# Layer 0 self attention of a four-layer decoder by half sequences, with 32-row and 32-column TensorE tiles

## The chip, the cores and the metric

The kernel runs on one core of a Trainium2 chip, in one launch. The metric is the device time of one execution in microseconds (us); lower is better. The profiled execution is one execution with the hardware profiler on, and its own time is given beside its span.

## The reference

A decoder of four layers works on `x` of shape (16, 128, 128): 16 sequences of 128 tokens with 128 channels, float32. Each layer has a self attention, a cross attention and a feed-forward stage, all of different kinds, with a layer norm before each stage and a residual after it. The change touches the first of the twelve stages alone. Cut to that stage (16 heads of width 8, causal softmax, and a decay that depends on the distance of two tokens and is multiplied in after the softmax):

```python
x = x + attn(layernorm(x))

def attn(x):
    q, k, v = split(x @ W_attn, 3)             # (16, 128, 128) each, 16 heads of 8
    S = q @ k.T / sqrt(8)                      # per sequence and head, 128 x 128
    P = softmax(where(causal, S, -inf))
    y = (P * decay) @ v                        # decay is lower triangular, a constant
    return concat_heads(y) @ W_proj
```

## The kernel before

All 16 sequences lie in SBUF from start to end, tokens on the partitions, in G = 4 groups of GB = 4 sequences: `X[g]` is 128 x (4 x 128). The twelve stages run one after another. Each opens its own PSUM banks (eight in all, split into rings by name: `x`, `S`, `P`, `O`) and its own SBUF pools. Tiles come from rotating pools, and a framework puts in the semaphores. A scheduler of that framework fixes each engine's order of instructions when the kernel is built, so that every engine then works its own list strictly in order; the source order is not the order of the lists.

The stage is `l0_attn` (L470). `pre_norm` (L308) normalises all of `X`: statistics on VectorE (L286, L287), the scaling (L299), four transposes a group on TensorE (L276) and a copy out of PSUM on ScalarE (L317). Then, group by group:

- q and k for the whole group, channels on the partitions (L478), copied out by VectorE (L483, L485), and v, tokens on the partitions (L489, L497).
- For each sequence `expand_heads` (L462) makes `kexp` on GpSimd: the keys of the sequence, 16 times over, each copy with all channels but one head's set to zero (128 x 2048). With it one matmul over all 128 channels gives the scores of several heads at once.
- `small_head_attention` (L424) works a sequence in four units of 4 heads. In a unit TensorE puts the causal mask into a bank by a bfloat16 matmul (L433) and adds the scores (L440, 512 columns; a float32 matmul is two passes, each with a weight load). `softmax_unit` (L324) takes the row maximum on VectorE (`nmax`, L329) and four exponentials on ScalarE (L332), each with a running sum that is read out by an instruction of its own (ACTIVATION_READ_ACCUMULATOR). Four transposes on TensorE follow (L345), then the product with the decay on VectorE on the way out of PSUM (L348), then four matmuls with the transposed weights as the stationary operand and 8 columns of v as the moving one (L452).
- After the four units the division by the sums (L456, L503) and one transpose into `yT` (L509). After the four sequences the copy of `yT` (L511), the output projection (L514) and the residual (L322).

At the start of the program the bfloat16 constants, among them the causal mask, come through a wide float32 tile and a cast on GpSimd (L268); the scores wait for them.

Of the kernel before, what the change touches and what calls it, by code (L numbers as in the profile page):

```python
# [36 lines left out]
def _columns(sizes):  # L37
    at, out = 0, {}
    for name, n in sizes:
# [9 lines left out]
        ("decayT", 128),  # L49
        ("cumsum", 128),  # L50
        ("head8", 16),
        ("head16", 8),
        ("mod8", 8),
        ("head64", 2),
# [107 lines left out]
class Decoder:  # L162
# [145 lines left out]
    def pre_norm(self, transpose=True):  # L308
# [9 lines left out]
            xnT.append(dst)  # L318
        return xn, xnT

    def add_to_x(self, g, what):
        self.nc.vector.tensor_tensor(self.X[g], self.X[g], what, ALU.add)  # L322

# [143 lines left out]
        )  # L467
        return kexp

    def l0_attn(self, pool, _):  # L470
        nc = self.nc
        _, xnT = self.pre_norm()
        Wa, Wp = self.w["W_attn"], self.w["W_proj"]
        for g in range(G):
            qk = []
            for i in range(2):
                bank = self.ps()
                nc.tensor.matmul(  # L478
                    bank, lhsT=Wa[:, i * 128 : (i + 1) * 128], rhs=xnT[g], start=True, stop=True
                )  # L480
                sb = self.t(pool, (128, N), f"qk{i}")
                if i == 0:
                    nc.vector.tensor_scalar_mul(sb, bank, 1.0 / math.sqrt(8))  # L483
                else:
                    nc.vector.tensor_copy(sb, bank)  # L485
                qk.append(sb)
            v_ps = self.ps((T, GB, D))
            for b in range(GB):
                nc.tensor.matmul(  # L489
                    v_ps[:, b, :],  # L490
                    lhsT=xnT[g][:, b * T : (b + 1) * T],
                    rhs=Wa[:, 256:384],
                    start=True,
                    stop=True,
                )
            v = self.t(pool, (T, GB, D), "v")
            nc.vector.tensor_copy(v, v_ps)  # L497
            yT = self.ps()
            for b in range(GB):
                kexp = self.expand_heads(pool, qk[1], self.cst("head8"), b, 16)  # L500
                O, r = self.small_head_attention(pool, qk[0], kexp, v[:, b, :], b, True)
                y = self.t(pool, (T, D), "y")
                nc.vector.tensor_tensor(  # L503
                    y.rearrange("p (h d) -> p h d", h=16),
                    O,
                    r.unsqueeze(2).to_broadcast([T, 16, 8]),
                    ALU.mult,
                )
                nc.tensor.transpose(yT[:, b * T : (b + 1) * T], y, self.ident)  # L509
            yTs = self.t(pool, (D, N), "yT")  # L510
            nc.vector.tensor_copy(yTs, yT)  # L511
            o = self.ps((T, GB, D))
            for b in range(GB):
                nc.tensor.matmul(  # L514
                    o[:, b, :], lhsT=yTs[:, b * T : (b + 1) * T], rhs=Wp, start=True, stop=True
                )
            self.add_to_x(g, o)

    def context_T(self):
        for g in range(G):  # L520
# [882 lines left out]
    def run(self, stack):  # L1403
        self.setup(stack)
        with ExitStack() as inner:
            self.banks(inner, "c", x=8)
            self.context_T()
        heads = dict(x=2, S=2, P=2, O=2)
        moe = dict(x=2, S=2, P=2, O=2)
        todo = [  # L1410
            (self.l0_attn, 2, heads), (self.l0_xattn, 2, heads), (self.l0_ffn, 2, moe),
            (self.l1_attn, 2, heads), (self.l1_xattn, 2, heads), (self.l1_ffn, 2, dict(x=2, S=5, O=1)),
            (self.l2_attn, 2, dict(x=2, S=2, P=2, O=2)), (self.l2_xattn, 2, heads), (self.l2_ffn, 2, dict(x=3, S=3, O=2)),
            (self.l3_attn, 2, dict(x=2, S=4, O=2)), (self.l3_xattn, 2, dict(x=8)), (self.l3_ffn, 3, moe),
        ]
# [22 lines left out]
def constants():  # L1438
    import numpy as np

    p = np.arange(128)
    c = np.zeros((128, CONST_N), np.float32)
    half = np.zeros((128, HALF_N), np.float32)

    def put(name, a, columns=CONST, into=c):
        at, n = columns[name]
        a = np.asarray(a, np.float32).reshape(-1, n)
        into[: len(a), at : at + n] = a

# [8 lines left out]
    put("head8", p[:, None] // 8 == np.arange(16))  # L1458
    put("head16", p[:, None] // 16 == np.arange(8))
# [145 lines left out]
```

## Time and profile before

| | |
|---|---|
| runs, no profiler | 2403.79, 2404.2, 2407.95 us; median 2404.2 us |
| profiled execution, own time | 2406.38 us |
| its span in the trace | 2404.6 us |
| mean granted TensorE clock | 0.853 of full speed |
| busy share of the span | TensorE 81%, VectorE 58%, ScalarE 39%, GpSimd 24% |
| the stage in the trace | `kexp` of the first group starts at 31.51 us, the last residual of the stage (L322) at 246.42 us |
| instructions in the stage | 256 exponentials with 256 read-outs, 64 row maxima, 64 decay products, 16 `kexp` |

A busy time is the sum of the durations of the instructions of one engine, where overlaps count once. Matmuls are pipelined: the start of one to the start of the next says what it costs, and its duration is longer than that. PEclk is the TensorE clock that the throttle granted, as a share of full speed. What stands in brackets at the end of a row of the timeline is the engine's idle time before the row and what ended it.

### The profile page before, as it was taken

How to read it: one execution, taken by the hardware profiler on the slowest of the kernel's cores; microseconds unless marked ns; L12 is line 12 of the kernel's file. 1: busy time of each engine (PE TensorE's matmuls, PEld its weight loads, DVE VectorE, ACT ScalarE, POOL GpSimd, SP SyncE). 2: the span in 40 equal slices, each digit the busy share in tenths (PEclk: the TensorE clock that was granted, in tenths of full speed). 3: DMA queues.
4: the chain of work that ended last, by engine and by line, in shares of the span. 5: the costliest groups of instructions: out<-in, count | busy, mean ns of one | idle time of the engine just before them, and what ended most of it. 6: DMA issues, size and time to landing. Idle time of an engine off the chain costs nothing.

```text
span 2404.6 us, 25103 instructions
## 1 busy us (share of the span) xinstructions
PE 1941.3 (81%) x8660; PEld 1213.5 (50%) x8660; DVE 1387.8 (58%) x2650; ACT 936.6 (39%) x3012; POOL 569.6 (24%) x544
## 2 busy tenths in 40 slices
PE   6998787889889999977667668999964498328998
PEld 4666555357558887632212226777743355213443
DVE  4555365457656666456777764545455546884333
ACT  3444243246525555136343334445431143222333
POOL 2222131033200001415777752000001105610000
PEclk8888597869899999976887879999976677558999
DMA  4000000000000000000000000000000000000000
GB/s 147 1 1 1 1 1 1 33 3 1 1 1 1 1 1 29 2 0 0 1 0 1 0 33 1 1 1 1 1 31 0 0 1 0 0 0 0 5 5 9
DMA packets 11890, 19.08 MB, mean 8 GB/s; under 512 B 1499, under 2 KB 8795, under 8 KB 11379
## 3 DMA queue, kind: packets, MB, share of 16 engines
q1 hardware_dynamic: 11763, 17.49, 2.1%
q8 instruction: 68, 1.11, 0.2%
q14 instruction: 59, 0.48, 0.1%
HBM read 16.30 MB, written 1.05 MB: 7 GB/s over the span
## 4 chain that ended last, share of the span: by engine, by line
PE 67%; DVE 14%; POOL 9%; issue 6%; ACT 2%; DMA 0%; POOLq 0%; DVEq 0%; ACTq 0%; SPq 0%
PE ps_P L345 6%; POOL hC L1030 6%; PE ps_O L414 5%; PE ps_S L440 5%; PE ps_O L452 5%; PE ps_O L756 5%; PE ps_S L745 5%; PE ps_S L406 4%; DVE hs L1028 2%; PE ps_O L1031 2%; DVE xn L299 2%; PE ps_S L743 2%; PE ps_O L763 1%; PE ps_x L1109 1%; PE ps_x L854 1%
## 5 line engine op out<-in xcount | busy, mean ns | idle before, releaser
L332 ACT ACTIVATE P<-ps_S,nmax 128x128 f32<-128x128 f32 x1024 | 362.0, 367 | 295.9 <-DVE nmax L329 294.3
L329 DVE TENSOR_REDUCE nmax<-ps_S 128x4 f32<-128x512 f32 x256 | 176.5, 691 | 138.9 <-PE ps_S L745 77.9
L1031 PE MATMUL ps_O<-hC,consts 128*128 128x512 f32 x256 | 177.5, 794 | 93.6 <-POOL hC L1030 83.3
L1030 POOL TENSOR_TENSOR hC<-hs,Cw 128x512 f32<-128x512 f32 x128 | 205.3, 1622 | 91.8 <-DVE hs L1028 50.2
L332 ACT ACTIVATION_READ_ACCUMULATOR P<-ps_S,nmax 128x1 f32 x1024 | 209.1, 204 | 0.0
L1028 DVE TENSOR_TENSOR_SCAN hs<-dA,dBx 128x512 f32<-128x512 f32 x128 | 162.8, 1309 | 71.4 <-POOL dA L1024 71.4
L350 DVE COPY PT<-ps_P 128x512 f32<-128x512 f32 x224 | 154.1, 688 | 85.8 <-PE ps_P L345 84.3
L345 PE MATMUL ps_P<-consts,P 128*128 128x128 f32 x1024 | 200.8, 288 | 1.3 <-ACT P L332 0.7
L413 DVE TENSOR_TENSOR ehg<-eh,ps_P 128x512 f32<-128x512 f32 x128 | 86.6, 687 | 143.9 <-PE ps_P L411 99.4
L345 PEld LDWEIGHTS ps_P<-consts,P 128*128 128x128 f32 x1024 | 137.3, 158 | 53.7 <-ACT P L332 44.9
L408 ACT ACTIVATE eh<-ps_S,params 128x512 f32<-128x512 f32 x128 | 87.5, 687 | 184.7 <-PE ps_S L406 142.3
L1031 PEld LDWEIGHTS ps_O<-hC,consts 128*128 128x128 f32 x256 | 47.2, 224 | 192.4 <-POOL hC L1030 124.3
L745 PE MATMUL ps_S<-kexp,q 128*128 128x256 f32 x512 | 141.0, 381 | 0.0
L414 PE MATMUL ps_O<-ehg,w 128*128 128x512 f32 x256 | 136.4, 630 | 4.0 <-DVE ehg L413 4.0
L756 PEld LDWEIGHTS ps_O<-v,PT 128*128 128x128 f32 x1024 | 127.1, 191 | 19.8 <-DVE PT L350 13.5
L406 PE MATMUL ps_S<-xnT,w 128*128 128x512 f32 x256 | 133.3, 610 | 0.0
L756 PE MATMUL ps_O<-v,PT 128*128 128x64 f32 x1024 | 131.6, 271 | 0.2 <-DVE PT L350 0.2
L1022 ACT ACTIVATE dA<-dt,A 128x512 f32<-128x512 f32 x128 | 92.4, 722 | 83.5 <-DVE hs L1028 83.4
L1138 POOL TENSOR_TENSOR q_v<-q_v,q_e 128x512 f32<-128x512 f32 (+3 forms) x10 | 21.1, 2120 | 436.4 <-DVE q_e L1137 436.4
L322 DVE TENSOR_TENSOR x<-x,ps_x 128x512 f32<-128x512 f32 x32 | 21.9, 684 | 145.6 <-PE ps_x L1191 46.5
L745 PEld LDWEIGHTS ps_S<-kexp,q 128*128 128x128 f32 x512 | 87.0, 192 | 16.0 <-issue 3.2
L276 PE MATMUL ps_x<-consts,xn 128*128 128x128 f32 x176 | 42.0, 397 | 61.0 <-DVE xn L299 57.8
(395 smaller groups left out, 3831.7 us busy)
## 6 DMA issues: line engine op xcount, KB each, us to landing
w<-in_w_dram SPq DMA_DIRECT2D x2, 1792.0 KB
wide_consts<-in_half_dram SPq DMA_DIRECT2D x1, 1554.0 KB
x<-in_x_dram SPq DMA_DIRECT2D x4, 256.0 KB
c<-in_ctx_dram SPq DMA_DIRECT2D x4, 256.0 KB
w<-in_Wq_dram SPq DMA_DIRECT2D x2, 512.0 KB
w<-in_Wo_dram SPq DMA_DIRECT2D x2, 512.0 KB
out_dram<-x SPq DMA_DIRECT2D x4, 256.0 KB
consts<-in_consts_dram SPq DMA_DIRECT2D x1, 748.0 KB
```

The lines of the kernel that those rows point to most:

```text
L329: nc.vector.tensor_reduce(nmax, S, AX.X, ALU.max, negate=True)
L332: nc.scalar.activation(P[:, j, :], S[:, j, :], AF.Exp, bias=nmax[:, j : j + 1], accum_out=sums[:, j : j + 1],)
L345: nc.tensor.transpose(PT[:, j, :], P[:, j, :], self.ident)
L350: nc.vector.tensor_copy(out, PT)
L406: nc.tensor.matmul(h_ps, lhsT=W1(c), rhs=xnT[g], start=True, stop=True)
L414: nc.tensor.matmul(acc, lhsT=W2(c), rhs=hg, start=False, stop=c == chunks - 1)
L440: nc.tensor.matmul(S, lhsT=q[:, b * T : (b + 1) * T], rhs=kexp[:, 4 * u : 4 * u + 4, :], start=not causal, stop=True,)
L745: nc.tensor.matmul(S[:, 2 * c : 2 * c + 2, :], lhsT=q[:, c, b * T : (b + 1) * T], rhs=kexp(c), start=bias is None, stop=bias is None or c ...
L756: nc.tensor.matmul(O[:, j, :], lhsT=PT[:, j, :], rhs=v(j), start=True, stop=True)
L1028: nc.vector.tensor_tensor_scan(h, dA, dBx, 0.0, ALU.mult, ALU.add)
L1030: nc.gpsimd.tensor_tensor(hC, h, Cw, ALU.mult)
L1031: nc.tensor.matmul(ysum[c], lhsT=self.ident, rhs=hC, start=n == 0, stop=n == 15)
```

## The change

The stage is rewritten; the eleven others keep their code and the order of their instructions.

- The unit is now half a sequence, 8 heads: unit n has sequence n // 2 and half p = n % 2, so there are 32 units. `kexp` is a quarter as wide (128 x 512): the mask `quarter8` repeats every 32 channels, so that channels 32r to 32r+31 hold the keys of heads 4r to 4r+3, one head in each copy.
- `scores`: two banks, one for each quarter r of the heads. The mask goes into both, and then the scores by two matmuls on 32 rows each, at row positions 64p and 64p+32.
- The exponentials have no running sum. GpSimd adds the two halves of each row of the weights (`half_sums`, 128 x 512 out) and the halves of that (`quarter_sums`, 128 x 256 out); VectorE reduces the rest (`sums`, in `back`).
- `turn`: eight transposes and two decay products. `values`: eight matmuls with 32 columns of `vaug` as the stationary operand (8 of them v, 24 zero) and the transposed weights as the moving one (128 columns), each into its own 32 partitions of the bank `O`; ScalarE copies `O`. `back`: two transposes bring it back to tokens on the partitions, and VectorE divides.
- `pipelined` issues the steps of different units in turn, with TensorE's list in that written order; the other engines' lists stay the scheduler's. In iteration i the order is scores(i), turn(i-1), values(i-2), back(i-3), ahead(i), gather(i-4), out(i-5). `ahead` makes the next group's transposes, q, k and v in the iterations 3 to 6 of a group (of eight), and `gather` and `out` act for the last unit of a group alone.
- q, k and v are copied out by ScalarE, and two `vaug` buffers (128 x 2048 each) are zeroed by GpSimd at the start. The stage's rings go from x=2, S=2, P=2, O=2 to x=1, S=4, P=2, O=1.

```diff
+    def pipelined(self, units, order):
+        with self.tc.manual_schedule(engines={mybir.EngineType.PE}):
+            for i in range(len(units) + max(late for _, late in order)):
+                for k, late in order:
+                    if 0 <= i - late < len(units):
+                        units[i - late][k]()
...
+            def scores():
+                if p == 0:
+                    self.kexp = self.expand_heads(pool, k[g], self.cst("quarter8"), b, 4)
+                S = [self.ps((T, 4, T), "S") for r in range(2)]
+                for r in range(2):
+                    nc.tensor.matmul(
+                        S[r], lhsT=self.half["ident"], rhs=causal, start=True, stop=True,
+                        skip_group_check=True,
+                    )
+                for r in range(2):
+                    rows = slice(64 * p + 32 * r, 64 * p + 32 * r + 32)
+                    nc.tensor.matmul(
+                        S[r],
+                        lhsT=q[g][rows, cols],
+                        rhs=self.kexp[rows, :, :],
+                        start=False,
+                        stop=True,
+                        tile_position=(64 * p + 32 * r, 0),
+                        skip_group_check=True,
+                    )
+                nmax = self.t(self.small, (T, 2, 4), "nmax")
+                own["P"] = P = self.t(self.deep, (T, 2, 4, T), "P")
+                for r in range(2):
+                    nc.vector.tensor_reduce(nmax[:, r, :], S[r], AX.X, ALU.max, negate=True)
+                    for j in range(4):
+                        nc.scalar.activation(
+                            P[:, r, j, :], S[r][:, j, :], AF.Exp, bias=nmax[:, r, j : j + 1]
+                        )
+                half = self.t(self.deep, (T, 8, 64), "half_sums")
+                Ph = P.rearrange("p r j k -> p (r j) k")
+                nc.gpsimd.tensor_tensor(half, Ph[:, :, 0:64], Ph[:, :, 64:128], ALU.add)
+                quarter = self.t(self.deep, (T, 8, 32), "quarter_sums")
+                nc.gpsimd.tensor_tensor(quarter, half[:, :, 0:32], half[:, :, 32:64], ALU.add)
...
+            def values():
+                O = self.ps((128, 2, T), "O")
+                for r in range(2):
+                    for j in range(4):
+                        nc.tensor.matmul(
+                            O[32 * j : 32 * j + 32, r, :],
+                            lhsT=vaug[g % 2][:, b, 8 * p + 4 * r + j, :],
+                            rhs=own["PT"][:, r, j, :],
+                            start=True,
+                            stop=True,
+                        )
+                own["OT"] = self.t(self.deep, (128, 2, T), "OT")
+                nc.scalar.copy(own["OT"], O)
+            def back():
+                Y = self.ps((T, 2, 4, 32))
+                for r in range(2):
+                    nc.tensor.transpose(
+                        Y[:, r, :, :].rearrange("p j d -> p (j d)"), own["OT"][:, r, :], self.ident
+                    )
+                sums, rec = self.t(self.small, (T, 8), "sums"), self.t(self.small, (T, 8), "rsum")
+                nc.vector.tensor_reduce(sums, own["quarter"], AX.X, ALU.add)
+                nc.vector.reciprocal(rec, sums)
...
-            (self.l0_attn, 2, heads), (self.l0_xattn, 2, heads), (self.l0_ffn, 2, moe),
+            (self.l0_attn, 2, dict(x=1, S=4, P=2, O=1)), (self.l0_xattn, 2, heads), (self.l0_ffn, 2, moe),
```

The lists of the built kernel show where the scheduler put the rest. On VectorE a unit's instructions stand as `nmax`(n) twice, the decay products of unit n-1, the division of unit n-3, `sums`(n), its reciprocal, `nmax`(n+1). In units 7 to 9, 15 to 17, 23 to 25, 29 and 30 the reciprocal follows the first `nmax`(n+1) or comes later; in units 2, 10, 18 and 26 the first `nmax`(n+1) stands ahead of `sums`(n). On ScalarE they stand as eight exponentials of unit n, the copy of `O` of unit n-2, then one of the copies for the next group. On GpSimd `half_sums`(n) and `quarter_sums`(n) stand together, with a `kexp` after every second pair or so; ahead of the first pair stand three `kexp`, the cast of the constants and the zeroing of both `vaug`.

More of the change, by code (lines that the diff above doesn't have):

```diff
@@ L51 @@
         ("head8", 16),
+        ("quarter8", 4),
+        ("pick", 4),
         ("head16", 8),
@@ L319, in pre_norm, with pre_norm_by_group, make @@
         return xn, xnT
+    def pre_norm_by_group(self):
+        nc = self.nc
+        mv, rstd = self.stats(self.X, 1e-5)
+        xn, xnT = [], []
+        def make(g):
+            xn.append(self.t(self.normed, (T, GB, D), f"xn{g}"))
+            xnT.append(self.t(self.normed, (D, N), f"xnT{g}"))
+            for b in range(GB):
+                i = g * GB + b
+                nc.vector.tensor_scalar(
+                    xn[g][:, b, :],
+                    self.X[g][:, b, :],
+                    mv[:, i, 0:1],
+                    rstd[:, i : i + 1],
+                    ALU.subtract,
+                    ALU.mult,
+                )
+            nc.scalar.copy(xnT[g], self.transposed(xn[g]))
+        return xn, xnT, make
+    def pipelined(self, units, order):
[4 more added lines that the diff above has]
+                        units[i - late][k]()
     def add_to_x(self, g, what):
@@ L468, in expand_heads, with l0_attn, project @@
         return kexp
-    def l0_attn(self, pool, _):
+    def l0_attn(self, pool, hold):
         nc = self.nc
-        _, xnT = self.pre_norm()
         Wa, Wp = self.w["W_attn"], self.w["W_proj"]
[L474 to L477, printed above, removed]
+        xn, xnT, make = self.pre_norm_by_group()
+        vaug = [self.t(hold, (T, GB, 16, 32), f"vaug{i}") for i in range(2)]
+        for v in vaug:
+            nc.gpsimd.memset(v.rearrange("p b h d -> p (b h d)"), 0.0)
+        causal = self.half["causal"].unsqueeze(1).to_broadcast([T, 4, T])
+        q, k, y = [], [], []
+        def project(g, i):
+            bank = self.ps(kind="P")
+            if i < 2:
                 nc.tensor.matmul(
@@ L480, in l0_attn @@
                 )
-                sb = self.t(pool, (128, N), f"qk{i}")
+                dst = self.t(pool, (128, N), f"qk{i}")
                 if i == 0:
-                    nc.vector.tensor_scalar_mul(sb, bank, 1.0 / math.sqrt(8))
+                    nc.scalar.mul(dst, bank, 1.0 / math.sqrt(8))
                 else:
-                    nc.vector.tensor_copy(sb, bank)
-                qk.append(sb)
-            v_ps = self.ps((T, GB, D))
+                    nc.scalar.copy(dst, bank)
+                (q, k)[i].append(dst)
+                return
+            v = bank.rearrange("p (b h d) -> p b h d", b=GB, h=16)
             for b in range(GB):
                 nc.tensor.matmul(
-                    v_ps[:, b, :],
+                    v[:, b, :, :].rearrange("p h d -> p (h d)"),
                     lhsT=xnT[g][:, b * T : (b + 1) * T],
@@ L495, in l0_attn, with unit, turn @@
                 )
-            v = self.t(pool, (T, GB, D), "v")
-            nc.vector.tensor_copy(v, v_ps)
-            yT = self.ps()
             for b in range(GB):
-                kexp = self.expand_heads(pool, qk[1], self.cst("head8"), b, 16)
-                O, r = self.small_head_attention(pool, qk[0], kexp, v[:, b, :], b, True)
-                y = self.t(pool, (T, D), "y")
+                nc.scalar.copy(vaug[g % 2][:, b, :, 0:8], v[:, b, :, :])
+        def unit(n):
+            s, p = n // 2, n % 2
+            g, b = s // GB, s % GB
+            cols = slice(b * T, (b + 1) * T)
+            own = {}
+            def scores():
[31 more added lines that the diff above has]
+                nc.gpsimd.tensor_tensor(quarter, half[:, :, 0:32], half[:, :, 32:64], ALU.add)
+                own["quarter"] = quarter
+            def turn():
+                own["PT"] = self.t(self.deep, (T, 2, 4, T), "PT")
+                for r in range(2):
+                    bank = self.ps((T, 4, T), "P")
+                    for j in range(4):
+                        nc.tensor.transpose(bank[:, j, :], own["P"][:, r, j, :], self.ident)
+                    nc.vector.tensor_tensor(
+                        own["PT"][:, r, :, :],
+                        bank,
+                        self.cst("decayT").unsqueeze(1).to_broadcast([T, 4, T]),
+                        ALU.mult,
+                    )
+            def values():
+                O = self.ps((128, 2, T), "O")
+                for r in range(2):
+                    for j in range(4):
+                        nc.tensor.matmul(
[4 more added lines that the diff above has]
+                            stop=True,
+                        )
+                own["OT"] = self.t(self.deep, (128, 2, T), "OT")
+                nc.scalar.copy(own["OT"], O)
+            def back():
+                Y = self.ps((T, 2, 4, 32))
+                for r in range(2):
+                    nc.tensor.transpose(
+                        Y[:, r, :, :].rearrange("p j d -> p (j d)"), own["OT"][:, r, :], self.ident
+                    )
+                sums, rec = self.t(self.small, (T, 8), "sums"), self.t(self.small, (T, 8), "rsum")
+                nc.vector.tensor_reduce(sums, own["quarter"], AX.X, ALU.add)
+                nc.vector.reciprocal(rec, sums)
+                if p == 0 and b == 0:
+                    y.append(self.t(pool, (T, GB, D), "y"))
@@ L503, in l0_attn @@
                 nc.vector.tensor_tensor(
-                    y.rearrange("p (h d) -> p h d", h=16),
-                    O,
-                    r.unsqueeze(2).to_broadcast([T, 16, 8]),
+                    y[g][:, b, 64 * p : 64 * p + 64].rearrange("p (h d) -> p h d", h=8),
+                    Y.rearrange("p r j d -> p (r j) d")[:, :, 0:8],
+                    rec.unsqueeze(2).to_broadcast([T, 8, 8]),
                     ALU.mult,
                 )
-                nc.tensor.transpose(yT[:, b * T : (b + 1) * T], y, self.ident)
@@ L510, in l0_attn, with ahead @@
[L510 to L517, printed above, removed]
+            def ahead():
+                if g < G - 1 and n % 8 >= 3:
+                    if n % 8 == 3:
+                        make(g + 1)
+                    elif n % 8 < 7:
+                        project(g + 1, n % 8 - 4)
@@ new lines, in gather, with out @@
+            def gather():
+                if n % 8 == 7:
+                    own["yT"] = self.t(pool, (D, N), "yT")
+                    nc.scalar.copy(own["yT"], self.transposed(y[g]))
+            def out():
+                if n % 8 == 7:
+                    o = self.ps((T, GB, D))
+                    for i in range(GB):
+                        nc.tensor.matmul(
+                            o[:, i, :], lhsT=own["yT"][:, i * T : (i + 1) * T], rhs=Wp,
+                            start=True, stop=True,
+                        )
+                    self.add_to_x(g, o)
@@ L519, in context_T @@
+            return [scores, turn, values, back, ahead, gather, out]
+        make(0)
+        for i in range(3):
+            project(0, i)
+        self.pipelined([unit(n) for n in range(2 * B)], [(0, 0), (1, 1), (2, 2), (3, 3), (4, 0), (5, 4), (6, 5)])
     def context_T(self):
@@ L1458, in constants @@
     put("head8", p[:, None] // 8 == np.arange(16))
+    put("quarter8", p[:, None] // 8 % 4 == np.arange(4))
+    put("pick", p[:, None] % 32 == np.arange(4))
     put("head16", p[:, None] // 16 == np.arange(8))
```

## The prediction

> **What bounds the kernel now.** I read the page, then stretches of the first stage with the granted clock, then the order in time of one unit and of one change of group.
>
> ```profile
> core 0: us, PE busy (x) PEld busy (x) DVE busy (x) ACT busy (x) POOL busy (x), PEclk, DMA share, GB/s
> 40.00:75.00 35.00, 34.54 (x221) 26.10 (x219) 21.66 (x36) 22.28 (x120) 7.22 (x2) 0.99 0.01 1
> 75.00:95.00 20.00, 14.76 (x49) 8.66 (x49) 7.76 (x18) 2.53 (x14) 7.17 (x2) 0.67 0.00 0
> 95.00:130.00 35.00, 34.54 (x223) 26.16 (x222) 20.99 (x36) 21.54 (x116) 7.22 (x2) 1.00 0.01 1
> ```
>
> Inside a group TensorE is busy throughout at full clock; between groups there are some 17 us with ScalarE nearly idle and the clock at 0.67. One steady unit of 4 heads:
>
> ```profile
> start us, us, engine line op out<-in xcount [idle before <-releaser]
> 219.06 0.95 PE L452 MATMUL ps_O<-v,PT 128*128 128x8 f32 x8
> 219.33 0.69 DVE L329 TENSOR_REDUCE nmax<-ps_S 128x4 f32<-128x512 f32 x1 [0.45 <-PE ps_S L440]
> 219.87 0.63 PE L345 MATMUL ps_P<-consts,P 128*128 128x128 f32 x4
> 220.34 0.38 PE L433 MATMUL ps_S<-half_consts 128*128 128x512 bf16 x1
> 220.54 0.69 DVE L348 TENSOR_TENSOR PT<-ps_P,consts 128x512 f32<-128x512 f32 x1 [0.36 <-PE ps_P L345]
> 220.56 1.02 PE L440 MATMUL ps_S<-kexp,qk 128*128 128x512 f32 x2
> 221.42 0.95 PE L452 MATMUL ps_O<-v,PT 128*128 128x8 f32 x8
> ```
>
> The PE starts are its costs: values 0.81, transposes 0.47, mask 0.22, scores 0.86 (0.43 a pass), together 2.36: TensorE's own list bounds it. Two units are 4.72 us for 8 heads. The change of group is a chain without company:
>
> ```profile
> 76.73 1.06 PE L452 MATMUL ps_O<-v,PT 128*128 128x8 f32 x8 [0.57 <-DVE PT L348]
> 77.83 0.29 DVE L503 TENSOR_TENSOR y<-ps_O,rsum 128x128 f32<-128x128 f32 x1 [1.15 <-PE ps_O L452]
> 78.66 0.69 DVE L511 COPY yT<-ps_x 128x512 f32<-128x512 f32 x1 [0.54 <-PE ps_x L509]
> 79.41 2.08 PE L514 MATMUL ps_x<-w,yT 128*128 128x128 f32 x8 [0.78 <-DVE yT L511]
> 81.27 3.62 PE L478 MATMUL ps_x<-xnT,w 128*128 128x512 f32 x4
> 85.77 7.17 POOL L462 TENSOR_TENSOR kexp<-qk,consts 128x2048 f32<-128x2048 f32 x2 [28.62 <-DVE qk L485]
> 89.43 2.92 PE L440 MATMUL ps_S<-kexp,qk 128*128 128x512 f32 x3 [3.50 <-POOL kexp L462]
> ```
>
> The first `kexp` of the groups start at 31.51, 85.77, 140.15 and 194.65, so a group takes 54.4: sixteen units are 37.7, the change 16.7. The stage's last residual starts at 246.42; all later lists are the same before and after, so I ask when that residual starts.
>
> **What goes.** The three changes (3 x 16.7 = 50) are taken up by `ahead`, `gather` and `out`. The 256 read-outs go: exponentials start 0.345 apart with them, and 0.257 apart without ((1.14 - 0.37) / 3 in the first row below), so eight take 7 x 0.257 + 0.37 = 2.17.
>
> **What TensorE has to do for 8 heads.** Mask 2 x 0.22 = 0.43; eight transposes 0.94; two to bring back 0.24; the next group's and the output's work 4.6 us in 8 units (0.5 for `make`, 4 x 0.43 for q and k, 8 x 0.12 for v, 0.5 for `gather`, 8 x 0.12 for `out`), 0.58. Not in the trace are matmuls on part of the array. Scores: four passes one by one 1.72 (the nearest row, L440), both quarters wholly side by side 0.86. Values: sixteen passes of 128 columns at 0.117 (L345, the same length) 1.87, four side by side 0.47. Each matmul is two passes on one tile, and the next is on another, so if tiles can overlap only neighbours do: three pass times (1.29) and nine (1.05). I take these; the ends stay for the range. The tile shape changes four times a unit. A lone transpose at full clock lasts 0.27 (L509) against 0.12 in a stream, so emptying the array costs 0.14, 0 to 0.4 with the next load exposed: 4 x 0.14 = 0.56. The sum is 5.1; the ends are 3.5 and 7.4.
>
> The Trainium skill (TensorEngine Tiling (Array Packing), Tiling Modes) lets different tiles load and multiply in parallel, and its table gives up to 4 times for four tiles; no row here shows it, and by that rule the sum above would be near 3.5, an estimate. The same section says that changing the tiling mode drains TensorE, which speaks against this change; it gives no duration.
>
> **What the other engines have to do.** VectorE: two maxima and two products at 0.61 (start to start of 128x512 rows) and small ones, 3.4. ScalarE: 2.1, the copy of O 0.37 (L766, 128x256), copies for the next group 0.4: 2.9. GpSimd 2.2. None is as long as TensorE's 5.1. But VectorE's list puts `sums`(n) ahead of `nmax`(n+1), and that is a new loop through three engines. Its prices:
>
> ```profile
> 285.92 1.14 ACT L635 ACTIVATE decay<-ps_S,nM 128x128 f32<-128x128 f32 x4 [1.10 <-PE ps_S L625]
> 319.03 1.04 POOL L664 TENSOR_TENSOR sq<-h 128x512 f32<-128x512 f32 x1 [0.63 <-DVE h L660]
> 320.10 0.69 DVE L666 TENSOR_REDUCE ms<-sq 128x32 f32<-128x512 f32 x1 [0.55 <-POOL sq L664]
> ```
>
> First maximum 0.69, hand-over 0.04, exponentials 2.17 (the second maximum lies beside them), 0.07, `half_sums` 1.04, 0.07, `quarter_sums` 0.61 (`kexp` is 1.90 for 1024 and 3.61 for 2048: 1.67 ns an element and 0.19), 0.03 (L664 to L666), `sums` 0.41 (from 0.69 for 512 and, L1131, 1.62 for 1408), 0.03, reciprocal 0.18 (0.17 for 4, 0.24 for 16): 5.34. Where the reciprocal comes later, 5.1. I take 5.3. Behind the waiting `sums`(n) are queued the next maxima, and behind these ScalarE and TensorE's next transposes; the decay products are done. In units 10, 18 and 26 the first maximum has gone ahead and 1.1 is saved: 4.2.
>
> TensorE, at 5.1, keeps ahead of this loop, but with little to spare: the loop bounds by 0.2.
>
> **The sum.** Start: the constants arrive at 27.27 and are cast by 30.04, as before. TensorE begins at 30.1 at half clock. ScalarE's `vaug` copies wait for the zeroing (1.8, from 1.38 for 1536 columns) until 31.9, take 1.0, and its table load 1.28 comes after: first exponential 34.25 (38.01 now). Two units fill the pipeline; GpSimd's third `kexp` waits for unit 1's scores (37.5) and stands ahead of `half_sums`(0), so `sums`(0) comes at 40.3, `sums`(1) at 43.6, and unit 4's maxima at 50.1. Then 24 x 5.3 + 3 x 4.2 = 139.8 to unit 31. At a change of group `make`, `gather` and `out` share the one `x` bank with `back`: `make` waits for the division (2.9 into the loop), `gather` for ScalarE's copy, so the next scores are late by 1.0, and the residual with its statistics (0.69 and six small ones) stands ahead of the maxima one unit later, 1.7. That is 2.7, 2.7 and, without `make`, 1.75: 7.2. After the last maximum starts: exponentials 2.9, transposes 3.3, products 4.0, values 5.1, copy 5.6, back and division 6.3, transposes 7.0, copy 7.7, projection 8.9; 11 if the clock is at half by then, as it is now (0.53 from 238 to 248), which I take. Residual at 50.1 + 139.8 + 7.2 + 11 = 208.1, against 246.42: 38.3 less. The profiled execution's 2406.4 becomes 2368.1; it stood 2.2 above the median, so the median becomes 2365.9. A difference under 0.2% (4.8 us) can't be told from none.
>
> **Rivals.**
> - TensorE bounds: tiles one after another, 5.78 + 0.56 = 6.34 a unit. With 1.5 more at the start, 3 at the changes and 12 behind, 50.1 + 1.5 + 27 x 6.34 + 3 + 12 = 237.8: 9 less, 2395. For it: every pass in this trace stands alone. Against it: the instructions alternate tiles.
> - GpSimd in company: L1030, the same shape, takes 1.62 beside VectorE's scans. Then `half_sums` and `quarter_sums` cost 0.8 more, 27 x 0.8 = 22: 16 less, 2388. Against it: VectorE waits while they run.
> - Slower: tiles one after another and an empty array with an exposed load at each of four switches, 5.78 + 4 x 0.4 = 7.38. 66.6 + 27 x 7.38 = 265.9: 19 more, 2423 (66.6 is all of the last sum but the 27 units). It decides from (246.4 - 66.6) / 27 = 6.66 a unit. A granted clock that falls inside the loop would end on the same side.
> - The change doesn't do what it says: the scheduler's lists undo the pipeline. That is the loop that I have priced.
>
> **How the numbers follow.** Forecast 0.56 (2355 to 2380); TensorE bound 0.15; GpSimd 0.08; slower 0.17; the crossing near 6.66, no change, 0.04. Faster 0.79, same 0.04, slower 0.17. The low end is a loop of 5.0 and a tail at full clock (8 + 2 more, so 2354). The high end has to take in the first three cases and the crossing and so reaches 2410, leaving out most of the slower case.
>
> **What would show it.** In the profile after: first exponential near 34; `nmax` starts 5.3 apart with VectorE idle before `sums`, released by GpSimd; `half_sums` at 1.04; scores of a unit in 1.3 and values in 1.1; PEclk near 1.0 between 50 and 195; L356's last residual in the stage near 208. It is wrong if VectorE's long idle ends on TensorE, if GpSimd's adds are over 1.3, or if PEclk sits near 0.5.

## The result and the profile after

The changed kernel takes 2378.1 us (median of 8 runs, 2375.7 to 2383.0) against 2402.8 us of the kernel before, run on the same chip (8 runs, 2387.3 to 2411.0): a ratio of 0.9906, 95% interval 0.9881 to 0.9931. It is faster by about 25 us; 38 were forecast. The stage's last residual starts at 223.10, against 246.42 before and 208.1 forecast. These stage times are the sharper measure: behind that residual all kernels here run the same instructions, and the profiled executions still spend 2148.5 to 2163.4 us there (before 2158.2, after 2150.9). Of the 30.6 us between the two profiled spans, 23.3 are the change's.

One steady unit of 8 heads after the change, in order of time (start, duration, engine, line, operation, and in brackets the idle time before it with what ended it; of TensorE only the next unit's scores are shown):

```profile
57.26 1.25 DVE L571 TENSOR_REDUCE nmax<-ps_S 128x4 f32<-128x512 f32 x2
58.00 2.17 ACT L573 ACTIVATE P<-ps_S,nmax 128x128 f32<-128x128 f32 x8 [2.73 <-DVE nmax L571]
60.24 1.26 POOL L578 TENSOR_TENSOR half_sums<-P 128x512 f32<-128x512 f32 x1 [3.60 <-ACT P L573]
60.64 1.13 PE L559 MATMUL ps_S<-kexp,qk 32*128 32x512 f32 x4
61.58 0.73 POOL L580 TENSOR_TENSOR quarter_sums<-half_sums 128x256 f32<-128x256 f32 x1
62.35 0.42 DVE L617 TENSOR_REDUCE sums<-quarter_sums 128x8 f32<-128x256 f32 x1 [2.52 <-POOL quarter_sums L580]
62.80 0.20 DVE L618 RECIPROCAL rsum<-sums 128x8 f32<-128x8 f32 x1
62.92 1.25 DVE L571 TENSOR_REDUCE nmax<-ps_S 128x4 f32<-128x512 f32 x2
```

Read it as a ring, TensorE's row left aside. Each row waits for the one above, over three engines (the exponentials for the first of the two maxima), and VectorE's only long idle time (2.52) ends on GpSimd. The next unit's maxima, whose scores are done at 61.77, stand behind `sums` in VectorE's queue and start at 62.92. The starts are the terms: 0.74 + 2.24 + 1.34 + 0.77 + 0.45 + 0.12 = 5.66. That is the forecast ring, with the two GpSimd steps longer than forecast.

Three such stretches as in the views of the kernel before, a loop, a change of group and a loop again (time, then busy time and instructions of each engine, and the granted clock):

```profile
40.00:75.00 35.00, 30.72 (x242) 15.99 (x238) 20.23 (x47) 17.17 (x62) 16.69 (x17) 0.94 0.00 1
88.00:99.00 11.00, 7.08 (x38) 3.71 (x38) 3.96 (x11) 3.87 (x12) 4.94 (x5) 0.69 0.00 0
107.00:130.00 23.00, 18.30 (x147) 9.59 (x148) 13.42 (x32) 11.73 (x45) 10.96 (x11) 0.99 0.01 2
```

In the loop no engine is full any more: TensorE 30.7 of 35, where it had 34.5. At the change the clock falls to 0.69. What happens there, in order of time:

```profile
87.58 0.64 DVE L571 TENSOR_REDUCE nmax<-ps_S 128x4 f32<-128x512 f32 x1
90.40 0.68 DVE L571 TENSOR_REDUCE nmax<-ps_S 128x4 f32<-128x512 f32 x1
91.00 1.28 DVE L589 TENSOR_TENSOR PT<-ps_P,consts 128x512 f32<-128x512 f32 x2
92.20 0.21 DVE L621 TENSOR_TENSOR y<-ps_x,rsum 128x64 f32<-128x64 f32 x1
92.47 1.12 PE L278 MATMUL ps_x<-consts,xn 128*128 128x128 f32 x4 [3.25 <-DVE y L621]
93.62 0.58 ACT L342 COPY xnT<-ps_x 128x512 f32<-128x512 f32 x1 [1.10 <-PE ps_x L278]
94.26 1.12 PE L278 MATMUL ps_x<-consts,y 128*128 128x128 f32 x4 [0.68 <-ACT xnT L342]
96.16 2.08 PE L559 MATMUL ps_S<-kexp,qk 32*128 32x512 f32 x4
98.33 1.29 DVE L571 TENSOR_REDUCE nmax<-ps_S 128x4 f32<-128x512 f32 x2 [3.24 <-PE ps_S L559]
```

`make`'s transposes need the one `x` bank, and the division that frees it stands on VectorE behind the second maximum and two decay products. TensorE waits 3.25 with unit 12's scores behind it in its fixed list, then 0.68 more, and then runs at half clock: the scores take 2.08, in the loop 1.13. From the second maximum of unit 11 (90.40; its first had gone ahead at 87.58) to the maxima of unit 12 pass 7.9 us.

### The profile page after: what moved, and what is told of

Same layout as the page of the kernel before. It is cut to its first block, busy times and chain, and to the rows that moved or that the text cites. A ratio compares the mean times of both kernels' runs of the same rounds, so it can differ in the third digit from the quotient of the medians.

```text
span 2374.0 us, 25157 instructions
## 1 busy us (share of the span) xinstructions
PE 1896.8 (80%) x8691; PEld 1156.9 (49%) x8724; DVE 1380.9 (58%) x2698; ACT 928.8 (39%) x2816; POOL 596.2 (25%) x610
## 3 DMA queue, kind: packets, MB, share of 16 engines
q8 instruction: 69, 1.13, 0.2%
HBM read 16.31 MB, written 1.05 MB: 7 GB/s over the span
## 4 chain that ended last, share of the span: by engine, by line
PE 61%; DVE 15%; POOL 12%; issue 9%; ACT 2%; DMA 1%; SPq 0%; POOLq 0%; DVEq 0%; ACTq 0%
POOL hC L1168 6%; PE ps_O L448 5%; PE ps_S L883 5%; PE ps_O L894 5%; PE ps_P L379 5%; PE ps_S L440 5%; PE ps_O L486 3%; PE ps_S L474 3%; DVE hs L1166 2%; PE ps_O L1169 2%; DVE xn L301 2%; PE ps_S L881 2%; POOL half_sums L578 2%; PE ps_O L901 1%; PE ps_x L1247 1%
## 5 line engine op out<-in xcount | busy, mean ns | idle before, releaser
L366 ACT ACTIVATE P<-ps_S,nmax 128x128 f32<-128x128 f32 x768 | 271.6, 367 | 176.5 <-DVE nmax L363 175.2
L363 DVE TENSOR_REDUCE nmax<-ps_S 128x4 f32<-128x512 f32 x192 | 132.2, 690 | 97.3 <-PE ps_S L883 80.9
L379 PE MATMUL ps_P<-consts,P 128*128 128x128 f32 x768 | 156.7, 286 | 1.5 <-ACT P L366 0.7
L366 ACT ACTIVATION_READ_ACCUMULATOR P<-ps_S,nmax 128x1 f32 x768 | 157.1, 205 | 0.0
L379 PEld LDWEIGHTS ps_P<-consts,P 128*128 128x128 f32 x768 | 103.8, 156 | 46.5 <-ACT P L366 37.6
L573 ACT ACTIVATE P<-ps_S,nmax 128x128 f32<-128x128 f32 x256 | 69.8, 381 | 85.5 <-DVE nmax L571 73.8
```

Source lines behind the costliest of these rows:

```text
L363: nc.vector.tensor_reduce(nmax, S, AX.X, ALU.max, negate=True)
L366: nc.scalar.activation(P[:, j, :], S[:, j, :], AF.Exp, bias=nmax[:, j : j + 1], accum_out=sums[:, j : j + 1],)
L379: nc.tensor.transpose(PT[:, j, :], P[:, j, :], self.ident)
```

## The experiments

"Step" is the time from one unit's first maximum to the next one's, in units without work for the next group where nothing else is said. All ratios are to the kernel before, on the same chip.

**1. Late sums.** VectorE's order is written by hand too, so that `sums` of unit n stands behind the maxima of unit n+3. The reciprocal and the division of unit n move with it. `normalise` is the four L334 instructions, taken out of `make` and put two units ahead of it.

```diff
-        with self.tc.manual_schedule(engines={mybir.EngineType.PE}):
+        with self.tc.manual_schedule(engines={mybir.EngineType.PE, mybir.EngineType.DVE}):
...
+                if g < G - 1 and n % 8 == 1:
+                    normalise(g + 1)
```

> The changed kernel, with VectorE's order written by hand as well: `sums`, the reciprocal and the division of unit n stand behind the maxima and decay products of unit n+3, where the GpSimd adds have long been done; the normalising of the next group's rows is put two units ahead of its transposes. No instruction goes. Theory (the loop VectorE, ScalarE, GpSimd, VectorE bounds a steady unit): the first maxima are 5.66 apart now and come 4.0 to 4.4 apart, TensorE's own list (about 3.4 in the changed trace and up to 0.6 of the next group's work); 18 steady steps save 1.3 to 1.6 each and the changes of group some more, so the last residual of the stage comes at 185 to 198 instead of 223.1 and the time is 25 to 38 us under the changed kernel's. Rival (TensorE, at the 5.1 of the prediction, is close behind): 5.1 to 5.3 apart, residual at 212 to 216, 7 to 11 us less.

Steps of 3.45, and 4.69 with a projection; last residual 188.58; 2344.4 us, ratio 0.975 (0.9726 to 0.9774). No instruction went: the ring was the bound, and it came from the order of one queue, where one reduction stood ahead of the next maxima. TensorE's list for one such unit is now seen without a wait:

```profile
68.07 0.59 PE L555 MATMUL ps_S<-half_consts 128*128 128x512 bf16 x2
68.59 1.13 PE L561 MATMUL ps_S<-kexp,qk 32*128 32x512 f32 x4
69.65 1.09 PE L590 MATMUL ps_P<-consts,P 128*128 128x128 f32 x8
70.68 0.65 PE L602 MATMUL ps_O<-PT,vaug 128*32 128x128 f32 x16
71.25 0.44 PE L615 MATMUL ps_x<-consts,OT 128*128 128x128 f32 x2
71.53 0.38 PE L555 MATMUL ps_S<-half_consts 128*128 128x512 bf16 x1
```

From the starts: mask 0.52, scores 1.06, transposes 1.03, values 0.57, back 0.28, together 3.46, which is the step. The 4.0 to 4.4 expected was too high because it put work for the next group into every unit.

**2. The running sum back.** ScalarE sums each row itself; both GpSimd adds and VectorE's sum go.

```diff
-                            P[:, r, j, :], S[r][:, j, :], AF.Exp, bias=nmax[:, r, j : j + 1]
+                            P[:, r, j, :], S[r][:, j, :], AF.Exp, bias=nmax[:, r, j : j + 1],
+                            accum_out=sums[:, 4 * r + j : 4 * r + j + 1],
```

> The changed kernel with ScalarE's running sum back: each exponential reads its row sum out, and the two GpSimd adds and VectorE's sum of 32 go. Exponentials start 0.345 apart with the read-out, so eight take 7 x 0.345 + 0.37 = 2.8 instead of 2.17. Theory (the loop through GpSimd bounds): what is left of the loop is 0.74 + 2.8 + reciprocal 0.2 = 3.8, and TensorE's list 3.4 to 4.0, so steps of 3.8 to 4.2, residual at 183 to 198, 25 to 40 us less than the changed kernel. Rival (TensorE bounds at 5.1): residual at 212 to 216. Second rival (ScalarE's list with the read-outs bounds): 2.8 + 0.4 for the copy of O + 0.4 for the next group's copies = 3.6, which cannot be told from the theory here.

Steps of 3.78, last residual 186.00, 2346.6 us, ratio 0.9756 (0.9731 to 0.9782). The step is the ring without GpSimd, 3.8 as added up beforehand, and not TensorE's 3.46: VectorE's reciprocal waits for ScalarE's read-outs, ahead of the next maxima.

```profile
73.21 0.20 DVE L613 RECIPROCAL rsum<-sums 128x8 f32<-128x8 f32 x1 [1.10 <-ACT P L574]
```

That ScalarE's own list bounds, the second rival, could not be told apart here; experiment 9 runs at 3.46 with the same read-outs.

**3. One GpSimd add instead of two.**

```diff
-                nc.gpsimd.tensor_tensor(quarter, half[:, :, 0:32], half[:, :, 32:64], ALU.add)
...
-                nc.vector.tensor_reduce(sums, own["quarter"], AX.X, ALU.add)
+                nc.vector.tensor_reduce(sums, own["half"], AX.X, ALU.add)
```

> The changed kernel without the second GpSimd add: VectorE sums 64 columns of each head instead of 32. The loop loses `quarter_sums` and its hand-over (0.77 from its start to that of `sums`) and the sum grows from 0.42 to 0.69. Theory (the loop bounds, so that each term of it counts in full in each unit): steps of 5.66 - 0.77 + 0.27 = 5.16, 27 units x 0.5 = 13 less, residual near 210. Rival (something else bounds, TensorE for instance): less than 3 us either way. Rival (VectorE's own work bounds): 0.27 x 27 = 7 more.

Steps of 5.14 and 4.93, where the changed kernel has 5.67 and 5.46: each term of the ring counts in full. Last residual 211.51, 2367.7 us, ratio 0.9846 (0.9818 to 0.9873).

**4. Two `x` banks.**

```diff
-            (self.l0_attn, 2, dict(x=1, S=4, P=2, O=1)),
+            (self.l0_attn, 2, dict(x=2, S=3, P=2, O=1)),
...
-[(0, 0), (1, 1), (2, 2), (3, 3), (4, 0), (5, 4), (6, 5)]
+[(0, 0), (1, 1), (2, 2), (3, 3), (4, 0), (5, 5), (6, 6)]
```

> The changed kernel with two `x` banks and three `S` banks instead of one and four, and with `gather` and `out` one unit later each. The loop is untouched. At a change of group the next group's transposes (`make`) need not wait for the division of unit 8, nor `gather` for ScalarE's copy. Three steps around each change take 20.5, 20.4 and 20.4 now (from the first maximum of unit 10, 18, 26 to that of unit 13, 21, 29), against 3 x 5.5 = 16.5 for steady units. Theory (the one bank, and the clock that falls to half while TensorE waits for it, make the change dear): 17 to 18.5 each, so 6 to 10 less, residual at 213 to 217, granted clock above 0.9 between 75 and 110. Rival (the residual and its statistics on VectorE, and the output's matmuls, make it dear): 19.5 to 20.5 each, residual at 220 to 223. Rival (three `S` banks make the scores wait for exponentials): steps over 5.7, residual after 224.

The three steps take 16.2, 16.0 and 15.6. `out` comes one step later, so the fair stretch is four steps at the first two changes: 23.2 and 23.0, against 26.2 and 26.1. Last residual 212.71, 10.4 earlier; 2372.2 us, ratio 0.9871 (0.985 to 0.9893). At the first change `make`'s transposes start at 93.23, right behind those of `back`, where the changed kernel idles 3.25. So the wait for the one `x` bank was the larger part of what made the changes dear; `gather` and `out`, moved in the same edit, are not separated from it. The clock forecast was a miss: 0.85 between 75 and 110, 0.80 in the changed kernel. Three `S` banks cost nothing in the loop (5.46), but the second unit starts 4.58 after the first instead of 2.89: its second mask waits 1.52 for a bank that ScalarE still reads.

**5. Both, and the normalising at the start.** Late sums with all four groups normalised before the loop, and with the rings and order of experiment 4.

```diff
+        for i in range(G):
+            normalise(i)
         make(0)
...
-            (self.l0_attn, 2, dict(x=1, S=4, P=2, O=1)),
+            (self.l0_attn, 2, dict(x=2, S=3, P=2, O=1)),
```

> The kernel with VectorE's order by hand (`sums` three units late), with all four groups normalised at the start, where VectorE waits for constants, and with two `x` and three `S` banks and `gather` and `out` one unit later. Theory (what is left in that kernel is TensorE's list plus waits for the `x` bank and for VectorE's normalising): units without work for the next group stay 3.45 to 3.7 apart (three `S` banks may cost 0.2), those with a projection 4.7, and the steps of 7.0, 6.2, 8.7, 6.65 and 6.2 at the changes become 4 to 5. 27 units at 4.25 in the mean are 115, so the last residual comes at 170 to 178 instead of 188.6, and the time is 10 to 18 us under that kernel. Rival (the waits are made up elsewhere, by VectorE's 3.2 of work a unit): residual at 183 to 189.

Plain steps 3.51, at the changes 3.9 to 5.6; last residual 172.86; 2328.0 us, ratio 0.97 (0.9674 to 0.9726).

**6. The same with the old rings.** Four `S` banks and one `x`; `make`, `gather` (through `transposed`) and `out` use the `P` ring.

```diff
-        bank = self.ps()
+        bank = self.ps(kind=kind)
...
-                    o = self.ps((T, GB, D))
+                    o = self.ps((T, GB, D), "P")
```

> As the kernel with two `x` and three `S` banks, but with the rings of the changed kernel (one `x`, four `S`, two `P`, one `O`): the transposes of `make` and `gather` and the projection of `out` use the `P` ring instead of `x`. Theory (the `x` bank alone makes the changes dear): as there, 170 to 180; they wait for a decay product (0.3 to 0.9 each) instead, and four `S` banks keep 3.45 for the plain units. Rival (three `S` banks cost 0.2 a unit in the other): this one is 3 to 6 us earlier at the last residual; if they cost nothing, it is 1 to 4 us later.

Last residual 168.53, 4.3 earlier; 2326.8 us, ratio 0.968 (0.9643 to 0.9717). The rival had the size, but not the place: plain steps differ by 0.05, and from unit 5 to unit 31 both take the same (105.9 and 106.1). All of it lies ahead of unit 5: 0.65 already at the first maximum, 1.7 where the wait for a third bank falls in experiment 4 (4.58 against 2.89), the rest in the steps after that.

**7. Column tiles undone, with late sums.** The kernel of experiment 5, with its values as in the kernel before and the rings x=1, S=3, P=2, O=2.

```diff
-                            O[32 * j : 32 * j + 32, r, :],
-                            lhsT=vaug[g % 2][:, b, 8 * p + 4 * r + j, :],
-                            rhs=own["PT"][:, r, j, :],
+                            O[:, 4 * r + j, :],
+                            lhsT=own["PT"][:, r, j, :],
+                            rhs=vaug[g % 2][:, b, 8 * p + 4 * r + j, 0:8],
```

> The kernel with late sums, with the column tiles undone: eight matmuls a unit with the turned P as weights and 8 value columns moving, as in the kernel before; O needs no copy and no transposes to bring it back; rings one `x`, three `S`, two `P`, two `O`. TensorE loses 0.57 + 0.27 and gains 8 x 0.2 = 1.6 (0.81 for four in the trace of before). Theory (with the loop gone TensorE bounds, so that the column tiles are worth their TensorE time): units 4.1 to 4.3 instead of 3.45, 27 x 0.75 = 20, so the last residual 15 to 22 us after that of the same kernel with column tiles. Rival (VectorE, 3.2 a unit, or ScalarE bounds and TensorE has slack): less than 5 us later.

Where the clock is full, the step is 4.22, as forecast: values take 1.71 instead of 0.57 and 0.28.

```profile
152.53 1.85 PE L602 MATMUL ps_O<-vaug,PT 128*128 128x8 f32 x16
154.24 0.59 PE L555 MATMUL ps_S<-half_consts 128*128 128x512 bf16 x2
```

But the clock is mostly not full. Busy time by stretch, first this kernel, then that of experiment 5:

```profile
40.00:75.00 35.00, 35.00 (x129) 24.30 (x127) 13.91 (x28) 11.73 (x41) 10.69 (x12) 0.50 0.00 1
75.00:110.00 35.00, 35.00 (x129) 24.36 (x128) 13.13 (x28) 10.07 (x37) 10.49 (x11) 0.50 0.00 0
```

```profile
40.00:75.00 35.00, 34.77 (x268) 18.58 (x270) 24.85 (x51) 21.67 (x80) 19.13 (x20) 0.89 0.01 1
75.00:110.00 35.00, 34.62 (x306) 19.40 (x297) 29.15 (x69) 23.67 (x88) 21.45 (x22) 1.00 0.01 2
```

TensorE counts as busy in all of the 35 us, and the clock stays at 0.50; steps are 8 to 9.9. The last residual stands at 289.96, 117 later, where 15 to 22 were forecast. This kernel's twelve runs took 2366 to 2449 us, the longer the lower their mean clock (0.850 to 0.821); the profiled one took 2442. The five under 2400 us give a ratio of 0.9947 (0.9908 to 0.9985), still some 59 us more than experiment 5. At full clock the steps are 0.71 longer than in experiment 5, an estimated 19 us of the 59 in 27 steps; that the rest is clock too is not shown, as none of the five was profiled.

**8. One row tile for both score matmuls, with late sums.** The kernel of experiment 5 with one edit: the second quarter's scores are left out, and the first quarter's are computed twice.

```diff
-                    rows = slice(64 * p + 32 * r, 64 * p + 32 * r + 32)
+                    rows = slice(64 * p, 64 * p + 32)
...
-                        tile_position=(64 * p + 32 * r, 0),
+                        tile_position=(64 * p, 0),
```

> The kernel with late sums, with both score matmuls of a unit on one row tile: the second quarter's scores are left out, and the first quarter's are computed twice, from the same 32 rows. The matmuls, their columns and banks stay. Theory (two row tiles run wholly side by side, four passes of 0.43 in 1.06): on one tile the four passes take 1.72 to 1.9, units come 4.1 to 4.3 apart, and the last residual 18 to 22 us after that of the same kernel with two tiles. Rival of the prediction (only neighbouring passes overlap, 1.29): 0.4 to 0.5 a unit, 11 to 14 us. Rival (the passes of one matmul do not overlap another tile's, and the 1.06 has another cause): less than 3 us.

```profile
122.67 1.98 PE L561 MATMUL ps_S<-kexp,qk 32*128 32x512 f32 x4
124.58 0.33 PE L590 MATMUL ps_P<-consts,P 128*128 128x128 f32 x1
```

The scores take 1.91 from start to start, 1.06 on two tiles; steps of 4.31 instead of 3.51; last residual 195.99, 23.1 later; 2352.4 us, ratio 0.9801 (0.977 to 0.9831). The difference of 0.85 is two passes of 0.43: the two row tiles ran wholly side by side.

**9. Experiment 6 with the running sum.** The edit of experiment 2 on the kernel of experiment 6.

> The kernel with late sums and everything of `make`, `gather` and `out` in the `P` ring, with ScalarE's running sum back in place of the two GpSimd adds and VectorE's sum. ScalarE has 2.8 for eight exponentials with read-out and 0.42 for the copy of O, 3.2 a unit; VectorE 0.4 less than before; GpSimd only `kexp`. Theory (in that kernel TensorE's list of 3.45 bounds plain units, and the read-outs hide): plain units 3.45 to 3.6, last residual within 3 us of that kernel's, time within 4 us. Rival (ScalarE bounds: the hand-overs between maxima and exponentials are not hidden): plain units 3.7 to 3.9, as in the kernel with the running sum alone (3.78), last residual 5 to 10 us later.

Plain steps 3.46, last residual 166.62, 2320.6 us, ratio 0.9666 (0.9645 to 0.9687). The read-outs hide under TensorE. This is the lowest median measured, 79 us under the kernel before; its interval overlaps that of experiment 6.

**10. One row tile, in the changed kernel.** The edit of experiment 8 on the changed kernel itself.

> The changed kernel with one edit: both score matmuls of a unit on one row tile (the second quarter's scores left out, the first's computed twice). TensorE has 0.8 more to do in every unit, as measured where TensorE bounds. Theory (the loop through GpSimd bounds and TensorE, 3.45 and up to 0.7 for the next group, has 1.3 or more to spare): the scores are done later, but VectorE still waits for `quarter_sums`; plain steps stay 5.67 and 5.46, the last residual within 5 us of 223.1 (the scores count at the changes of group and in the start and tail). Rival (TensorE is close behind the loop, 5.1 as forecast): steps 5.9, 27 x 0.45 = 12 later, near 235.

Steps of 5.67 and 5.46, unchanged to the hundredth, with 0.8 more for TensorE in each. Last residual 228.84, 5.7 later, a little over the 5 expected: 2.0 up to unit 4, 2.9 from there to unit 31, where the scores count at the changes, and 0.9 in the tail. 2379.1 us, ratio 0.9918 (0.9894 to 0.9943).

**11. Column tiles undone, in the changed kernel.** The edit of experiment 7, and `gather` and `out` one unit later.

```diff
-            (self.l0_attn, 2, dict(x=1, S=4, P=2, O=1)),
+            (self.l0_attn, 2, dict(x=1, S=3, P=2, O=2)),
```

> The changed kernel with the column tiles undone as in the kernel with late sums (turned P as weights, 8 value columns moving; no copy and no transposes back), rings one `x`, three `S`, two `P`, two `O`, `gather` and `out` one unit later; to be held against the changed kernel with two `x` and three `S` banks (last residual 212.7). At full clock TensorE has 4.2 to 4.9 a unit, under the loop's 5.5. Theory (the loop bounds and hides it): steps stay 5.46 to 5.7, last residual 208 to 216. Rival (the granted clock: with matmuls of 8 columns and waits in each loop it stays at 0.5, as in the kernel with late sums and without column tiles, where TensorE was busy throughout at 0.50): units of 8 to 9.9, last residual 270 to 300, over 50 us later; or between the two, if the clock comes and goes.

The clock came and went: 0.50 from 40 to 75 with TensorE busy 35.00 of 35 and steps of 8 to 9.9, then steps of 4.2 from unit 7 to unit 10 at full clock. Last residual 276.74; six runs took 2381 to 2436 us. This is the clock rival's result. The theory could not be put to the test, though: with `y` read from another bank the scheduler wrote VectorE's list anew and put `sums` behind the next unit's first maximum, where it waits 0.2 to 0.4 for GpSimd instead of 2.5:

```profile
98.03 0.69 DVE L571 TENSOR_REDUCE nmax<-ps_S 128x4 f32<-128x512 f32 x1 [0.84 <-PE ps_S L559]
99.11 0.42 DVE L610 TENSOR_REDUCE sums<-quarter_sums 128x8 f32<-128x256 f32 x1 [0.39 <-POOL quarter_sums L580]
```

So at full clock there was no ring left to hide under, and the 4.2 is TensorE's.

**12. Another pair of inputs for the first GpSimd add.**

```diff
-                nc.gpsimd.tensor_tensor(half, Ph[:, :, 0:64], Ph[:, :, 64:128], ALU.add)
+                nc.gpsimd.tensor_tensor(half.rearrange("p h k -> p (h k)"), Pf[:, 0:512], self.cst("zero_first"), ALU.add)
```

> The changed kernel, with the inputs of the first GpSimd add changed: 512 adjoining columns of P and 512 adjoining constants instead of two sets of eight runs of 64 columns; what it sums is then not the row sums. The add is the same size: 1.27 in the changed kernel, forecast as 1.04 from a row whose two inputs are the same tile. If the runs of 64 columns make it dear: 1.04 to 1.10, steps of 5.45 instead of 5.67. If two separate inputs make it dear: 1.27, steps unchanged.

This add, the add of the changed kernel, and two rows of before (minimum, median and longest in ns, first and last start):

```profile
L579 POOL TENSOR_TENSOR half_sums<-P,consts x32: 1265/1272/1279, 35.5 to 195.1; 128x512 f32<-128x512 f32 x32
```

```profile
L578 POOL TENSOR_TENSOR half_sums<-P x32: 1261/1266/1279, 37.7 to 215.7; 128x512 f32<-128x512 f32 x32
```

```profile
L1275 POOL TENSOR_TENSOR st<-st,q x16: 1257/1266/2097, 1994.6 to 2060.2; 128x512 f32<-128x512 f32 x16
L664 POOL TENSOR_TENSOR sq<-h x4: 1038/1038/1039, 319.0 to 406.6; 128x512 f32<-128x512 f32 x4
```

The runs of 64 columns are not what is dear: adjoining columns take 1.27 too. L1275 multiplies two different tiles and takes 1.27 in the median, L664 one tile by itself and takes 1.04. Two separate tiles are not dear in themselves either: `kexp` of the changed kernel (L496, 128x512) reads two, both broadcast, and takes 1.04. The steps, though, fell from 5.67 to 4.66, which neither reading had forecast. The new input is only the first half of P, so that the add starts after four exponentials instead of eight: 4 x 0.257 = 1.03 less, once more a term of the ring that counts in full. The units that took 5.46 take 4.66 too, as their reciprocal stands ahead of the next maximum in this kernel's list.

## Why the prediction was right, and where it fell short

The stretch from unit 4's maxima to unit 31's is 51.59 to 212.70, 161.1, where 147.0 were forecast. The four parts of the sum:

| part | forecast | measured | difference |
|---|---|---|---|
| unit 4's maxima | 50.1 | 51.6 | +1.5 |
| 18 plain steps | 95.4 (5.3) | 99.8 (5.54) | +4.4 |
| 9 steps at the changes | 51.6 | 61.4 | +9.8 |
| tail | 11 | 10.4 | -0.6 |

The median, 2378.1, lies 2 us inside the upper end of the forecast's own case (2355 to 2380) and 10 under the rival of dear GpSimd adds (2388). The time alone would not have told the two apart; the steps and the experiments do. The low end's sum, 8 + 2 under 2365.9, is 2356 and not 2354.

- **The ring.** Right, and shown by experiments 1, 2, 3 and 12: it sets the step, term by term. Mis-sized were `half_sums` (1.11 with its hand-over, measured 1.34) and `quarter_sums` (0.64, measured 0.77); the other four terms together came to 3.55 against 3.59. The step that failed is the choice of row: L664 has the shape, but reads one tile twice, and `kexp`, from which `quarter_sums` was priced, has two broadcast inputs. L1275, in the same trace, reads two tiles and has the price of `half_sums`. The rival of 1.62 in company did not come: the 32 adds are between 1261 and 1279 ns. (1.62 is the mean of L1030, which also reads two tiles; its median is 1.27.)
- **Changes of group.** This is the larger miss. The wait of `make` for the division was named, but priced at 1.0 for TensorE, at full clock. At the first change it waits 3.25 and 0.68 and then runs at half clock. With the forecast's 1.1 saved by the first maximum ahead, and plain steps of 5.54, the changes cost 5.2, 5.1 and 4.7 (stretches of four, four and five steps: 26.2, 26.1 and 31.3), 15.0 where 7.2 were forecast. Experiment 4, with a second bank and `gather` and `out` a unit later, takes 9.0 away between units 4 and 31.
- **TensorE.** 5.1 was forecast, of which 0.58 was work for the next group; the rest, 4.5, is 3.46 in experiment 1. That only neighbouring passes overlap was wrong: the scores (1.06 against 1.72 one by one) ran wholly side by side, by experiment 8, and so did the values, by their 0.57, where four side by side would be 0.47 and one by one 1.87. The 0.56 for the changes of tile shape fits, but was not tried by itself: the passes wholly side by side, 0.43 + 0.86 + 0.94 + 0.47 + 0.24 = 2.94, leave 0.52 for them and for all else. The error did no harm to the time, as the ring hides TensorE; experiment 10 shows that even 0.8 more a unit would have been hidden. "Little to spare" was wrong: it is 5.5 against 4.0 with the next group's work. The TensorE rival, tiles one after another, did not come.
- **The clock.** Forecast near 1.0 between 50 and 195; the mean was 0.86. It fell to half for 10 to 17 us at each change (92 to 102, 140 to 150, 188 to 204). A clock that falls inside the loop was named as another way to be slower and given no price. It came, for 3 to 7 us in plain units (82 to 85, 130 to 133, 174 to 181), and cost nothing there, as the steps stayed 5.46; in experiments 7 and 11, without the column tiles, half clock held for most of the stage.
- **The lists.** The rival that the scheduler's lists undo the pipeline was counted as the ring itself, and that is what came.
- **Start, tail, the rest.** First exponential 34.54 (forecast 34.25). The tail was taken at half clock; it had that only from 215 to 218, and full clock behind it. That 10.4 came out near 11 is in part luck: TensorE's list has work of units 29 and 30 and a matmul of the next stage (L756, at 217.86) ahead of unit 31's values (218.42), which no term covers. The rest of the program ran 7.3 us quicker in the profiled execution after than in the one before, which no term covers.

The Trainium skill (TensorEngine Tiling (Array Packing), Tiling Modes) says that different tiles work in parallel and that a change of mode drains TensorE. Experiments 1 and 8 agree with the first, with 1.06 for the scores on two tiles and 1.91 on one, and bound the second here: all that a unit's five pieces take beyond their passes is 0.52.

## What to carry to other kernels

A scheduler may put a small reduction whose input comes over two other engines ahead of the next unit's first instruction, and so make a ring out of a pipeline; its place in that one queue, moved in experiment 1 with the division and the normalising, was worth 35 us of the stage here, more than the whole change. Price an operation from a row with the same pattern of inputs, not only the same shape. At the places where a pipeline takes in a new group, list who holds each shared buffer, and what stands ahead of its release on that engine.

## What the runs showed of the hardware

- A busy TensorE is not enough for the full clock. With 8-column matmuls in the list it was busy 35.00 of 35 at a granted 0.50, for 70 us on end (experiment 7), while in experiment 10 TensorE, busy 34.13 of the 35 from 40 to 75, had 0.96 there (0.76 in the next 35, with a change of group). What the throttle follows instead is not shown: the kernel before kept 0.99 in its loop with 8-column matmuls too. The Trainium skill (TensorE: Matmul & The Clock Gate, Part 1: The HAM clock gate) has the clock released after about 3.4 us of sustained activity; what the profile calls busy is, by these runs, not that activity.
- VectorE's normalising of four 128x128 blocks took 2.41 beside the GpSimd adds (experiment 1, L333, at 76.57) and 4.19 for sixteen, so 1.05 for four, while GpSimd was idle (after, L334). Of the four, the two beside the adds took 1.09 and 0.89, the two behind them 0.33 each. The step that holds them took 5.63 instead of 3.45.
- GpSimd's 128x512 operation took 1.04 or 1.27 by its inputs: 1.27 in the median with two different full tiles, adjoining or in runs of 64, and 1.04 with one tile twice (L664) or with two broadcast ones (L496).
